# A vision tower's last feed-forward layer: one hand-written round an image, with its matrix products sorted by form

## The chip, the cores and the metric

The program runs on one core of one Trainium2 chip. The time is that of the whole program on the device, in microseconds (us), from start to end of one execution. Three executions of the kernel before took 1974.23, 1974.34 and 1977.2 us; their median is 1974.34. A further execution was taken with the hardware profiler: 1978.17 us, of which the span from the first to the last instruction is 1976.5.

The engines have short names here. PE is TensorE, which multiplies matrices; PEld is its loading of the stationary operand; DVE is VectorE, ACT is ScalarE, POOL is GpSimd; SP issues DMAs. Each engine works through its own list of instructions in order and waits at semaphores for the others. PE writes its results to PSUM, which has 8 banks of 128 x 512 numbers of 32 bits; ACT and DVE read them from there.

## What is computed

The program cuts 32 images of 3 x 256 x 256 into 256 tokens of 256 numbers each and sends them through two layers of attention and feed-forward. All numbers are float32. The change concerns the last part alone, the feed-forward of layer 1, which is itself a small attention with four heads (`NH`) and four experts (`NE`) a head:

```python
def _L1_ffn_ref(x, ...):                      # x: normalised tokens of all images
    sx = einsum('bsh,ndh->bnsd', x, hl_w) + hl_b          # 4 heads of 64
    q = einsum('bnsd,neod->bneso', sx, wq)                # one query per expert
    k = einsum('bnsd,nod->bnso', sx, wk)
    v = einsum('bnsd,nod->bnso', sx, wv)
    scores = einsum('bnesd,bntd->bnest', q, k) * d ** 0.5 + causal
    att = softmax(scores, axis=-1)
    qkv = einsum('bnest,bntd->bnesd', att, v)
    out = transpose(qkv, (0, 1, 3, 2, 4)).reshape(b, nh, s, ne * d)
    gs = softmax(einsum('bnsf,nef->bnse', out, gate_w) + gate_b, axis=-1)
    mixed = einsum('bnsed,bnse->bnsd', out.reshape(b, nh, s, ne, d), gs)
    resid = sx[arange(nh), arange(nh)]
    fx = layernorm(mixed + resid) ...                     # per head of 64
    hx = relu(fx @ fc1_w.T + fc1_b) @ fc2_w.T + fc2_b
    fout = layernorm(hx + fx, fnorm_g, fnorm_b)
    fg = softmax(fout @ fgate_w.T, axis=-1)
    return fout * fg                                      # added to the stream
```

## The kernel before

The kernel keeps all 32 images' tokens on the chip (`H`, one tile an image) and does the stages one after the other. The last stage, the feed-forward, begins at about 1275 us and ends the program. It takes one image after the other, cut into small pieces, and the pieces of several images are interleaved, so that every engine has something to do while an image's own chain waits.

What happens to an image, in order:

- `prep` -1 normalises the tokens (DVE, tile `ex`), `prep` 0 turns them feature-major (four transposes on PE, a copy to `exT` on ACT), `prep` 2 makes the heads `sx` (PE products with `w_hl`, two copies on ACT) and sends a copy with the two halves of partitions exchanged, `sw`, by two DMAs of SP. For the first four images it also makes `res`, the residual of the reference.
- `experts` multiplies the heads with `A` (query and key weights in one) and `experts_out` copies the result to `g` on ACT; `head_values` and `head_values_out` make the values `ev`; `prep` 7 also counts zeros.
- `scores` makes the scores in six steps k of two banks each; `weights` takes the exponentials of those banks on ACT (tiles `et`) and clears later keys by `affine_select` on POOL.
- `values` multiplies exponentials and values, 192 passes on PE an image in three groups, and copies eight results to `eo` on ACT.
- `post` 0 to 3: the gate's softmax, its mix of the experts (two multiplications of 128 x 1024 numbers on POOL, for the last two images on DVE), the sum and the residual `er`. `post` 15, 4, 5: a square on ACT, its sum on DVE, the power -1/2 on POOL (`head_rstd`, tile `hv`), the product on DVE. `post` 6 transposes it on PE, `post` 7 is the product with `fc1`, followed by four DMAs to the tile `both`, `post` 8 the product with `W2`. `post` 9, 10, 11, 12, 13 and 14 normalise, gate, transpose back, add and store. `post` 16 counts zeros, `post` 17 checks ranges for the last image.

All PE instructions have one helper, `mm` (L115), so the profile tells them apart by tiles. They come in three forms. *Full* products use all 128 rows and columns of PE's array: heads, `fc1`, all transposes. *Column halves* have 128 rows and 64 result columns; two such products run side by side in the two halves: `values` and `W2`. *Row halves* have 64 rows (one head of 64 is summed over) and 128 columns, also two side by side: `experts`, `head_values`, `scores`. A float32 product is two passes in the trace, a transpose one.

The order is written out by hand, for all engines. A step t does, for every image with a piece due, first the scores and experts of that step, then the early pieces, the exponentials, the other pieces by the tables `EARLY` and `PIECES`, and then the values; an image begins every six steps, so six steps are a round. `END` lists the pieces left after the last image. A bank is taken by `bank()`, in turn from a pool of eight, so the taker waits for the release of the bank taken eight times earlier.

Of the kernel before, what the change touches and what calls it, by code (L numbers as in the profile page):

```python
# [40 lines left out]
P = 128  # L41
# [38 lines left out]
def vit_tower(tc, a, out):  # L80
# [931 lines left out]
    with (  # L1012
# [4 lines left out]
        class Image:  # L1017


            def __init__(self):  # L1020
                self.p, self.t = {}, {}
# [4 lines left out]
        def prep(b, im, i):  # L1026
            if i == -1:
                im.x = normed_e(p1, b)
            if i == 0:
                im.xT = features(p1, im.x)  # L1030
            if i == 2:
                im.sx = p2.tile([P, 2, N], F32, name="sx")
                p = bank()
                for hp in range(2):
                    for k in range(2):
                        mm(p[:, hp * N : (hp + 1) * N], hl[:, k, hp * P : (hp + 1) * P], im.xT[:, k, :], k == 0, k == 1)
                for hp in range(2):
                    nc.scalar.activation(
                        im.sx[:, hp, :], p[:, hp * N : (hp + 1) * N], AF.Identity, bias=col("hl_b", hp)
                    )  # L1040

                im.sw = p2.tile([P, 2, N], F32, name="sw")
                for h in range(2):
                    nc.sync.dma_start(im.sw[halves[1 - h], :, :], im.sx[halves[h], :, :])
                im.g = p2.tile([P, NH, 2, N], F32, name="g")
                if b < NH:
                    p = bank()
                    for c in range(NC):
                        for k in range(2):
                            mm(  # L1050
                                p[:, c * HD : (c + 1) * HD], im.xT[:, k, c * P : (c + 1) * P],
                                hl[:, k, b * HD : (b + 1) * HD], k == 0, k == 1,
                            )
                    nc.vector.tensor_tensor(
                        res[:, :, b, :], p[:, 0 : NC * HD].rearrange("p (c d) -> p c d", c=NC),
                        over(row_e("hl_b")[:, b * HD : (b + 1) * HD], [P, NC, HD], 1), ALU.add,
                    )
                if b == NH - 1:
                    centred(res8, res8, NC * NH)
            if i == 7:  # L1060
                head_values_out(im)
                count_zeros(im.sx, b)
# [7 lines left out]
        def experts(im, hp):  # L1070


            ps = [bank(), bank()]
            for j in range(2):
                for s, p in zip(halves, ps):
                    mm(p[:, j * N : (j + 1) * N], A[s, hp, j * P : (j + 1) * P], im.sx[s, hp, :])
            im.pg = hp, ps

        def experts_out(im):
            hp, ps = im.pg  # L1080
            for h, p in enumerate(ps):
                nc.scalar.copy(im.g[:, 2 * hp + h, :, :].rearrange("p j n -> p (j n)"), p)  # L1082

        def head_values(im):
            im.v = p2.tile([P, NC, NH, VC], F32, name="ev")
            im.pv = [bank(), bank()]
            for c in range(NC):
                for hp in range(2):
                    o = (2 * c + hp) * VC
                    for s, p in zip(halves, im.pv):  # L1090
                        mm(p[:, o : o + VC], im.sx[s, hp, c * P : (c + 1) * P], WV[s, hp, :])

        def head_values_out(im):
# [7 lines left out]
        def scores(im, k):  # L1101


            if k == 4:
                im.o = p2.tile([P, NC * NH, 360], F32, name="eo")
# [10 lines left out]
        def weights(im, k):  # L1116

            hp, part = k // 3, k % 3
            for i, p in enumerate(im.p[k]):
# [4 lines left out]
                own = t[:, :, 0:P]  # L1124
# [4 lines left out]
                for h in range(2) if part == 2 else (part,):  # L1129
                    for j in range(2):  # L1130
                        im.t[2 * hp + h, 2 * j + i, part == 2] = t[:, 2 * (part // 2) * h + j, :]

        def values(im, j):
            for n, c in (((0, 0), (1, 0), (0, 1)), ((1, 1), (2, 0), (3, 0)), ((2, 1), (3, 1)))[j]:
                p, o = bank(), 0
                for e in range(NE):
                    x, w = TAKE[e]
                    for m in range(c + 1):
                        t = im.t[n, e, True] if m else im.t[n, e, False][:, c * P : (c + 1) * P]
                        for q in (slice(0, HD), slice(HD, P)):  # L1140
                            mm(p[q, o : o + w], t[:, q], im.v[:, m, n, x : x + w], m == 0, m == c)
                    o += w
                nc.scalar.copy(im.o[:, c * NH + n, 0:OC], p[:, 0:OC])  # L1143
# [38 lines left out]
        def post(b, im, i):  # L1182
# [37 lines left out]
            if i == (17 if b == B - 1 else 10) and b % 8 == 7:  # L1220
                check_ranges(b)
            if i == 5:
                nc.vector.tensor_tensor(im.r, im.r, over(im.rs, G8, 2), ALU.mult)
            if i == 6:
                p = feature_major(im.r.rearrange("p (c n) d -> p c (n d)", c=NC))
                im.fT = p1.tile([P, 2, N], F32, name="fxT")
                nc.scalar.activation(
                    im.fT.rearrange("p k n -> p (k n)"), p, AF.Identity, bias=col("e_b"), scale=col("e_g")
# [3 lines left out]
            if i == 7:  # L1232
                p = bank()
                mm(p, fc1, im.fT.rearrange("p k n -> p (k n)"))
                im.hx = p1.tile([P, 2, N], F32, name="hx")
                nc.scalar.activation(im.hx.rearrange("p k n -> p (k n)"), p, AF.Relu, bias=col("fc1_b"))
# [6 lines left out]
            if i == 8:  # L1243
                im.y = p2.tile([P, NC * NH, YC], F32, name="ey")
                for c in range(NC):
                    p = bank()
                    for n in range(NH):
                        for q in halves:
                            x = im.both[:, n % 2, n // 2, c * P + q.start : c * P + q.stop]
                            mm(p[q, n * YC : (n + 1) * YC], x, W2[:, n, :])  # L1250
                    nc.vector.tensor_tensor(
# [16 lines left out]
            if i == 12:  # L1268
                p = feature_major(im.r.rearrange("p (c n) d -> p c (n d)", c=NC))
                im.fT = p1.tile([P, 2, N], F32, name="foT")  # L1270
                nc.scalar.activation(
                    im.fT.rearrange("p k n -> p (k n)"), p, AF.Identity, bias=col("fn_b"), scale=col("fn_g")
# [24 lines left out]


        images = [Image() for _ in range(B)]
        SCORES, VALUES, LAST = 6, 11, 12  # L1300
        EARLY = ((32, post, 9), (22, post, 15))
        PIECES = (
            (24, post, 5), (0, prep, 0), (36, post, 12), (30, post, 16), (18, post, 1),
            (25, post, 6), (7, prep, 7), (31, post, 8), (19, post, 2),
            (38, post, 13), (2, prep, 2), (26, post, 7),
            (39, post, 14), (33, post, 10), (21, post, 3),
            (34, post, 11),
            (23, post, 4), (17, post, 0), (-1, prep, -1),
        )


        END = (
            (1, 1), (4, 12), (4, 13), (1, 2), (3, 16), (0, 0), (2, 5), (2, 6), (1, 3),
            (1, 15), (0, 1), (3, 8), (2, 7), (1, 4), (3, 9), (0, 2), (1, 5), (3, 10),
            (2, 16), (1, 6), (0, 3), (0, 15), (2, 8), (1, 7), (0, 4), (3, 11), (3, 12),
            (0, 5), (2, 9), (4, 14), (2, 10), (1, 16), (0, 6), (1, 8), (1, 9), (0, 7),
            (2, 11), (1, 10), (3, 13), (3, 14), (0, 16), (0, 8), (0, 9), (0, 10), (2, 12),
            (1, 11), (2, 13), (1, 12), (0, 11), (0, 17), (2, 14), (1, 13), (0, 12), (1, 14),
            (0, 13), (0, 14),
        )  # L1320

        def pieces(t, table):
            for step, do, i in table:
                b, r = divmod(t - step, 6)
                if r == 0 and 0 <= b < B:
                    do(b, images[b], i)

        order = tc.manual_schedule(engines={ENG.PE, ENG.DVE, ENG.Activation, ENG.Pool, ENG.SP})
        with order:
            for t in range(-1, 6 * (B - 1) + LAST):  # L1330
                active = [(images[b], t - 6 * b) for b in range(B)]
                if t % 2 == 0:
                    step = [(im, i - SCORES) for im, i in active if SCORES <= i < SCORES + 6]
                    made = [(im, i // 2 - 2) for im, i in active if i in (4, 6)]
                    for im, k in step:
                        scores(im, k)
                        scores(im, k + 1)
                    for im, hp in made:
                        experts(im, hp)
                    for im, i in active:  # L1340
                        if i == 6:
                            head_values(im)
                    pieces(t, EARLY)
                    for im, k in step:
                        weights(im, k)
                        weights(im, k + 1)
                    for im, hp in made:
                        experts_out(im)
# [401 lines left out]
```

## Time and profile before

| | us |
|---|---|
| median of three runs | 1974.34 |
| the profiled execution | 1978.17 |
| its span | 1976.5 |
| PE busy | 1933.4 (98%) |
| DVE busy | 1217.1 (62%) |
| POOL busy | 932.5 (47%) |
| ACT busy | 828.0 (42%) |
| start of the heads' products of image 5 | 1359.8 |
| of image 31 | 1888.8 |
| last score product | 1913.36 |

From image 5 to image 31 a round takes (1888.8 - 1359.8) / 26 = 20.35 us.

How it is read: busy time is the union of an engine's instructions. For PE the end of an instruction is modelled, and instructions overlap in the pipeline, so a share of 98% doesn't say that its array is well used; the distance from one start to the next is what counts. PE runs at full clock in the stage and at a lower mean (0.64) after the last score product, where it often waits.

### The profile page before, as it was taken

How to read it: one execution, taken by the hardware profiler on the slowest of the kernel's cores; microseconds unless marked ns; L12 is line 12 of the kernel's file. 1: busy time of each engine (PE TensorE's matmuls, PEld its weight loads, DVE VectorE, ACT ScalarE, POOL GpSimd, SP SyncE). 2: the span in 40 equal slices, each digit the busy share in tenths (PEclk: the TensorE clock that was granted, in tenths of full speed). 3: DMA queues.
4: the chain of work that ended last, by engine and by line, in shares of the span. 5: the costliest groups of instructions: out<-in, count | busy, mean ns of one | idle time of the engine just before them, and what ended most of it. 6: DMA issues, size and time to landing. Idle time of an engine off the chain costs nothing.

```text
span 1976.5 us, 37770 instructions
## 1 busy us (share of the span) xinstructions
PE 1933.4 (98%) x15108; PEld 1374.1 (70%) x15108; DVE 1217.1 (62%) x3225; ACT 828.0 (42%) x1549; POOL 932.5 (47%) x1072
## 2 busy tenths in 40 slices
PE   9999999999999999999999999999999999999984
PEld 7887676767666767666555555577787777778773
DVE  2335556566676655334565564536788878878886
ACT  0001312222222121222434444367777777777762
POOL 1223224343433343244334334247878787777862
PEclk9999999999999999999999999999999999999995
DMA  8550001000000142121000000001212122121212
GB/s 293 153 159 1 0 17 33 16 22 11 22 14 19 43 136 79 54 70 43 15 8 0 1 1 0 6 18 34 66 45 66 45 54 57 45 66 45 66 39 60
DMA packets 69668, 95.02 MB, mean 48 GB/s; under 512 B 8560, under 2 KB 51056, under 8 KB 69104
## 3 DMA queue, kind: packets, MB, share of 16 engines
q1 hardware_dynamic: 62768, 74.98, 13.4%
q0 software_dynamic: 6144, 16.79, 2.7%
q8 instruction: 121, 1.98, 0.4%
q10 hardware_dynamic: 576, 0.79, 0.1%
q14 instruction: 59, 0.48, 0.1%
HBM read 46.38 MB, written 20.97 MB: 34 GB/s over the span
## 4 chain that ended last, share of the span: by engine, by line
PE 94%; DVE 3%; POOL 1%; DMA 1%; ACT 1%; issue 0%; SPq 0%; ACTq 0%; DVEq 0%
PE bank L115 88%; PE bank L750 2%; PE bank L188 1%; PE bank L1279 1%; POOL eo L1205 0%; POOL hv L1157 0%; DMA patch<-in_patches_dram 0%; PE bank L229 0%; PE bank L482 0%; POOL et L1125 0%; DVE eo L1205 0%; DMA out_dram<-ex 0%; DVE six L123 0%; DVE h L827 0%; DMA sw<-sx 0%
## 5 line engine op out<-in xcount | busy, mean ns | idle before, releaser
L1125 POOL TENSOR_SCALAR_AFFINE_SELECT et<-et 128x256 f32<-128x256 f32 (+1 forms) x384 | 238.0, 651 | 34.2 <-ACT et L1122 32.4
L115 PEld LDWEIGHTS bank<-ev,et 128*64 128x64 f32 x6144 | 197.5, 136 | 33.2 <-issue 22.9
L115 PE MATMUL bank<-ev,et 128*64 128x74 f32 (+1 forms) x6144 | 210.2, 226 | 0.0
L1122 ACT ACTIVATE et<-bank 128x512 f32<-128x512 f32 x384 | 198.2, 604 | 21.4 <-PE bank L115 17.7
L115 PE MATMUL bank<-g,sx 64*128 64x512 f32 (+1 forms) x512 | 191.0, 502 | 1.4 <-ACT g L1082 1.4
L115 PE MATMUL bank<-g,sw 64*128 64x512 f32 (+1 forms) x512 | 190.0, 502 | 0.2 <-DMA sw<-sx 0.2
L115 PE MATMUL bank<-tokW,patch 128*128 128x256 f32 x768 | 168.9, 383 | 2.3 <-DMA patch<-in_patches_dram 2.3
L115 PEld LDWEIGHTS bank<-tokW,patch 128*128 128x128 f32 x768 | 147.6, 193 | 24.0 <-issue 3.2
L1205 POOL TENSOR_TENSOR eo<-eo,gate 128x1024 f32<-128x1024 f32 x60 | 114.3, 1927 | 102.3 <-DVE sm_m L1168 94.4
L115 PE MATMUL bank<-bxT,w_wuv 128*128 128x512 f32 x300 | 131.4, 592 | 0.0
L1143 ACT COPY eo<-bank 128x286 f32<-128x286 f32 x256 | 95.4, 404 | 68.0 <-PE bank L115 62.0
L148 POOL TENSOR_SCALAR rs_c<-st_c 128x4 f32<-128x4 f32 x16 | 3.1, 192 | 252.7 <-DVE st_c L124 252.7
L1157 POOL TENSOR_TENSOR hv<-hv,minus_half 128x8 f32<-128x8 f32 x64 | 119.2, 1862 | 5.3
L115 PE MATMUL bank<-wvo,dm 128*128 128x512 f32 x256 | 114.3, 599 | 0.0
L115 PE MATMUL bank<-w_wo,gT 128*128 128x256 f32 x512 | 113.1, 379 | 0.0
L115 PE MATMUL bank<-attn,bv 128*128 128x256 f32 x512 | 113.1, 379 | 0.0
L115 PE MATMUL bank<-w_w,hT 128*128 128x256 f32 x512 | 113.1, 379 | 0.0
L115 PE MATMUL bank<-xsel,w_w 128*128 128x512 f32 x256 | 111.4, 592 | 0.0
L115 PEld LDWEIGHTS bank<-attn,bv 128*128 128x128 f32 x512 | 97.2, 190 | 19.6 <-issue 6.7
L123 DVE BATCH_NORM_STATS2 six<-h 128x6 f32<-128x256 f32 x256 | 105.6, 413 | 4.4
L115 PEld LDWEIGHTS bank<-w_w,hT 128*128 128x128 f32 x512 | 96.6, 190 | 15.3 <-issue 2.9
L115 PEld LDWEIGHTS bank<-w_wo,gT 128*128 128x128 f32 x512 | 97.2, 190 | 13.2
(268 smaller groups left out, 3832.0 us busy)
## 6 DMA issues: line engine op xcount, KB each, us to landing
patch<-in_patches_dram SPq DMA_DIRECT2D x31, 768.0 KB, 4.5
sw<-sx SPq DMA_DIRECT2D x64, 128.0 KB, 2.4
both<-fxT SPq DMA_DIRECT2D x64, 128.0 KB, 2.2
both<-hx SPq DMA_DIRECT2D x64, 128.0 KB, 2.4
out_dram<-fout SPq DMA_DIRECT2D x29, 256.0 KB, 2.5
cs<-ranked SPq DMA_DIRECT2D x32, 128.0 KB, 2.0
results<-cy SPq DMA_DIRECT2D x32, 128.0 KB, 1.7
w_w<-in_w_dram SPq DMA_DIRECT2D x2, 1024.0 KB
```

The costliest lines, as they stand in the source:

```text
L115: nc.tensor.matmul(o, lhsT, rhs, start=first, stop=last)
L123: nc.vector.bn_stats(six, x)
L148: nc.gpsimd.tensor_scalar(o, var, 1.0, 1e-5, ALU.mult, ALU.add)
L188: nc.tensor.transpose(p[:, o : o + P], x[:, c, k * P : (k + 1) * P], ident)
L750: nc.tensor.transpose(p[:, o : o + P], x[:, c, k * P : (k + 1) * P], ident)
L1122: nc.scalar.activation(t, p, AF.Exp)
L1125: nc.gpsimd.affine_select(out=own, in_=own, pattern=[[0, n_e], [1, P]], compare_op=ALU.is_ge, fill=0.0, base=0, channel_multiplier=-1,)
L1143: nc.scalar.copy(im.o[:, c * NH + n, 0:OC], p[:, 0:OC])
L1157: nc.gpsimd.tensor_tensor(v, v, minus_half, ALU.pow)
L1205: (nc.vector if b > B - 3 else nc.gpsimd).tensor_tensor(im.mix[k], im.mix[k], over(im.gate[:, :, 2 * k : 2 * k + 2], [P, NC * NH, 2, HD], ...
L1279: nc.tensor.transpose(im.po[:, o : o + P], im.fT[:, k, c * P : (c + 1) * P], ident)
```

## The change

The pieces are cut finer, so that a product and the copy of its result are separate pieces, and their order is one table for a round of one image. The 59 pieces are numbered in the order in which an image needs them. `ROUND` names pairs (how many images back, piece); a round r does piece k for image r - back. PE's part of the table has all full products first (`post` 7 and 12, `post` 6 and 13, heads, the turn), then all on column halves (outputs 0 to 3, `post` 8, outputs 4 to 7), then all on row halves (experts 0, head values, experts 1, scores 2 to 5, and scores 0 and 1 of the next image). An image passes through nine rounds, from its tokens three rounds ahead to `post` 13 and 14 five rounds behind.

`weights` is split into `exponentials` (ACT) and `later_keys` (POOL), `values` into eight `outputs`, and `post` 6, 7, 8 and 12 into the PE part and a part 60, 70, 80 and 120 on ACT or DVE that reads the bank. The range check of the last image stands behind the hand-written order. What is computed, the number of instructions of each kind and the tiles' pools are the same.

```diff
-        def prep(b, im, i):
...
+        def turn(b, im):
+            im.pt = feature_major(im.x)
+
+        def turned(b, im):
+            im.xT = p1.tile([P, 2, N], F32, name="exT")
+            nc.scalar.copy(im.xT.rearrange("p k n -> p (k n)"), im.pt)
+
+        def heads(b, im):
+            p = im.ph = bank()
...
+        def heads_out(b, im):
+            im.sx = p2.tile([P, 2, N], F32, name="sx")
...
-        def weights(im, k):
-
+        def exponentials(b, im, k):
             hp, part = k // 3, k % 3
+            im.own[k] = []
             for i, p in enumerate(im.p[k]):
                 n_e = 4 if part == 2 else 2
                 t = pt.tile([P, 512], F32, name="et")
                 nc.scalar.activation(t, p, AF.Exp)
                 t = t.rearrange("p (e n) -> p e n", e=n_e)
-                own = t[:, :, 0:P]
+                im.own[k].append((t[:, :, 0:P], n_e))
...
+        def later_keys(b, im, k):
+
+            for own, n_e in im.own[k]:
                 nc.gpsimd.affine_select(
...
-        def values(im, j):
-            for n, c in (((0, 0), (1, 0), (0, 1)), ((1, 1), (2, 0), (3, 0)), ((2, 1), (3, 1)))[j]:
...
+        def outputs(b, im, j):
+            if j == 0:
+                im.o = p2.tile([P, NC * NH, 360], F32, name="eo")
+            n, c = ((0, 0), (1, 0), (0, 1), (1, 1), (2, 0), (3, 0), (2, 1), (3, 1))[j]
...
             if i == 6:
-                p = feature_major(im.r.rearrange("p (c n) d -> p c (n d)", c=NC))
+                im.pt = feature_major(im.r.rearrange("p (c n) d -> p c (n d)", c=NC))
+            if i == 60:
                 im.fT = p1.tile([P, 2, N], F32, name="fxT")
...
         PIECES = (
...
+            (tokens,), (turn,), (turned,), (heads,), (heads_out,), (experts, 0), (head_values,), (experts_out, 0),
+            (experts, 1), (experts_out, 1), (head_values_out,), (scores, 0), (scores, 1), (exponentials, 0),
+            (exponentials, 1), (heads_zero,), (later_keys, 0), (scores, 2), (scores, 3), (scores, 4), (scores, 5),
+            (exponentials, 2), (exponentials, 3), (exponentials, 4), (later_keys, 1), (exponentials, 5),
+            (later_keys, 2), (later_keys, 3), (outputs, 0), (outputs, 1), (outputs, 2), (outputs, 3),
+            (later_keys, 4), (outputs, 4), (outputs, 5), (later_keys, 5), (outputs, 6), (outputs, 7), (post, 0),
+            (post, 1), (post, 2), (post, 3), (post, 15), (post, 4), (post, 5), (post, 6), (post, 60), (post, 16),
+            (post, 7), (post, 70), (post, 8), (post, 80), (post, 9), (post, 10), (post, 11), (post, 12), (post, 120),
+            (post, 13), (post, 14),
         )
-
-
+        ROUND = (
+            (1, 39), (0, 24), (0, 25), (-3, 0), (-1, 13), (4, 54), (3, 48), (4, 55), (0, 26), (0, 27), (3, 49),
+            (-1, 14), (2, 44), (2, 45), (5, 57), (1, 40), (5, 58), (-2, 3), (2, 46), (-1, 15), (-3, 1), (4, 56),
+            (-2, 4), (0, 28), (0, 29), (-3, 2), (0, 30), (0, 31), (3, 50), (3, 51), (1, 41), (0, 32), (0, 33),
+            (0, 34), (0, 35), (3, 52), (0, 36), (3, 53), (0, 37), (-2, 5), (-2, 6), (-1, 16), (-2, 7), (0, 38),
+            (-2, 8), (-2, 9), (-1, 17), (-1, 18), (-2, 10), (1, 42), (-1, 19), (-1, 20), (2, 47), (-1, 21), (1, 43),
+            (-1, 22), (-1, 23), (-2, 11), (-2, 12),
+        )
...
+        LAST = PIECES.index((scores, 5))
+
+        def order_e():
+            for r in range(min(r for r, _ in ROUND), B + max(r for r, _ in ROUND)):
+                for back, k in ROUND:
+                    b = r - back
+                    if 0 <= b < B:
+                        yield b, k
+                        if (b, k) == (B - 1, LAST):
+                            yield from ((B - 1 - last, k) for last, k in END)
+                            return
+
+        with tc.manual_schedule(engines={ENG.PE, ENG.DVE, ENG.Activation, ENG.Pool, ENG.SP}):
+            for b, k in order_e():
+                do, *i = PIECES[k]
+                do(b, images[b], *i)
+        check_ranges(B - 1)
```

`END` has a new list of the pieces left after the last score product of image 31: 93 pairs of images 26 to 31, in place of 56.

## The prediction

> **What bounds the kernel now.** I read the shares first (PE 98%), then busy time by stretch, then the PE timeline of one round, then the rows of single tiles. By stretch (columns: stretch, length, busy of PE, PEld, DVE, ACT, POOL with instruction counts, granted clock, DMA share, GB/s):
>
> ```profile
> 1300.00:1880.00 580.00, 579.35 (x8924) 457.94 (x8922) 449.54 (x1072) 447.80 (x965) 438.35 (x508) 1.00 0.21 51
> 1502.26:1522.61 20.35, 20.35 (x316) 16.26 (x315) 17.42 (x41) 15.63 (x35) 15.12 (x19) 1.00 0.21 54
> 1913.36:1976.50 63.14, 32.02 (x384) 23.97 (x380) 45.30 (x124) 17.48 (x37) 18.26 (x20) 0.64 0.18 49
> ```
>
> The first line is the feed-forward in its steady part: PE lacks 0.65 us of 580. The second is one image: PE is full for all of its 20.35 us, at full clock, and DVE is next at 17.42. The third starts at the last product of a score and ends the run: there the last image's own chain decides, and PE is half idle. So from about 1275 to 1913 us the time is PE's list of work and nothing else; what shortens it must be in that list. The PE timeline shows what:
>
> ```profile
> 1506.72 0.43 PE L115 MATMUL bank<-ev,et 128*64 128x74 f32 x8
> 1507.08 0.69 PE L115 MATMUL bank<-g,sw 64*128 64x512 f32 x1
> 1507.61 0.59 PE L115 MATMUL bank<-g,sw 64*128 64x512 f32 x1
> 1508.05 0.38 PE L115 MATMUL bank<-g,sw 64*128 64x256 f32 x1
> ...
> 1521.18 0.59 PE L115 MATMUL bank<-g,sw 64*128 64x512 f32 x1
> 1521.60 0.59 PE L115 MATMUL bank<-g,sx 64*128 64x512 f32 x1
> 1522.13 0.55 PE L1279 MATMUL bank<-ident,foT 128*128 128x128 f32 x3
> ```
>
> Read the starts, since the ends are modelled. A pass of 512 columns takes 0.43 us (1507.61 to 1508.05, 1521.18 to 1521.60); the first pass after products of another form takes 0.53 (1507.08 to 1507.61), and the step from a row-half pass to a full transpose also takes 0.53 instead of 0.43. Nothing is waited for there; the change of form costs.
>
> **What the change removes.** Prices by kind, from starts in this round (first start after the change, plus what the second is late, each less the same step without a change):
> - full to column halves: 522 for 430 ns, then 115 for 64: 145 ns
> - column to row halves: 158 for 57, then 533 for 429: 205 ns
> - row to column halves: 306 for 209, then 115 for 64: 148 ns
> - row halves to full: 202 for 81, then 166 for 109 (178 ns); at the other place 520 for 422, then 165 for 109 (154 ns).
>
> An image has 2, 3, 1 and 2 of them: 290 + 615 + 148 + 332 = 1.385 us, so 18.96 of the 20.35 us are products. After the change it has one full to column (145), one column to row (205) and one row to full. That last one is followed by fc1's 512 columns; three rows early in the stage, where a wide full product follows a row half, show 519 for 422 and 320 for 216, so 200 ns. Sum 0.55. **A round without waits is 19.51 us, 0.84 less.** For the total I count changes of form in the order of PE's instructions, from the stage's first transpose to the last score product: 253 before (62 full-column, 93 column-row, 31 row-column, 64 row-full, 3 full-row), 96 after (31, 31, 0, 32, 2). That is 9.0 + 19.1 + 4.6 + 10.6 + 0.6 = 43.9 us against 4.5 + 6.4 + 6.4 + 0.4 = 17.7: **26.2 us saved.** The products themselves are the same, 5,297 in both.
>
> **What it moves.** Behind the last score product now lie one fc1 (2 x 0.43) and one set of foT transposes (4 x 0.11) more: 1.3 us leave the full part and go where PE is busy 32 of 63 us, at no cost. The last image's chain (exponentials, selects, eight outputs, post 0 to 14, the DMAs of `both`, out) has the same links; I keep its 63.1 us, with 4 to either side for the new order of the other images' pieces. The range check of the last image, now written after the hand order, was built in among DVE's waits before the last two stores: nothing, or its two operations of 0.64 us.
>
> Banks: the round takes 34 of them through 8 in turn. The densest part is the row halves, 18 banks in 0.86 + 0.90 + 0.86 + 6 x 0.86 = 7.8 us. At one place a rule speaks against this: the Trainium skill, "TensorEngine Tiling (Array Packing)", PSUM Bottleneck, warns that tiling speeds the products and not the emptying of PSUM. By the rule ACT would set the row part. By rows: after the second expert product ACT has two copies of `g` (0.47 apart), one square (0.47 more) and then exponentials 0.48 apart (four in 2.04 at 604 each, with one 0.2 us gate). Its eighth ends 6 us after that product; the transposes of post 6, which take that bank up again, come 6.66 us after it. Slack 0.6 us or more; I go by the rows: 0.
>
> SP's queue keeps seven issues an image: `sw` is sent by the heads' copies and read by scores 0 at the end of the same round's row part, some 12 us later (it landed in 2.4); `both` has the transposes of that round and the first outputs of the next, about 5 us against 2.4. POOL: selects 4 and 5 stand behind post 2's two mixes (3.8 us), so they end some 6 us after the heads' first product; outputs 6, their last reader, start at about 8 (heads 1.73, turn 0.44, four outputs and post 8). Nothing for either.
>
> **The wait that it adds** is DVE's. In the new order post 15 (the square) stands on ACT after the second experts' copies, and DVE then has post 4, post 1, the next normalisation, post 11 and only then post 5, which PE's post 6 needs. Count from the end of the second expert product. ACT: 0.2 latency + 0.47 + 0.47 + 0.63 = 1.77. DVE: reduce 0.67, add, max, subtract 0.56, two `ex` 0.82, `enorm` 0.69, `lg` 0.18 to 0.39, four small ones 0.71 to 1.01, `er` 0.69 to 1.1: from 4.3 to 5.3, with the medians of the rows 5.0. Ready at 6.1 to 7.0, likely 6.8. PE gets there after six score pairs (5.16), a change (0.20), fc1 (0.86) and post 12 (0.44): 6.66. The wait is 0 to 0.4 us a round. Its size hangs on DVE's rows beside POOL:
>
> ```profile
> L1223 DVE TENSOR_TENSOR er<-er,hv x32: 680/876/884, 1333.9 to 1942.3; 128x512 f32<-128x512 f32 x32
> L1170 DVE TENSOR_TENSOR fgate<-fgate,sm_m x32: 160/1735/1740, 1377.5 to 1967.0; 128x8 f32<-128x8 f32 x32
> L1289 DVE TENSOR_TENSOR fout<-fout,h x29: 691/1037/1131, 1381.2 to 1966.0; 128x512 f32<-128x512 f32 x29
> ```
>
> (minimum/median/maximum ns). An eight-column multiply takes 1735 ns because it stands beside POOL's mix of 1927. The Trainium skill, "SBUF — State Buffer", SBUF: two separate sides, says that a DVE operation with two SBUF inputs and a GpSimd one exclude each other for the whole instruction. By the rule `er`, which in the new order meets the 512-column selects of `later_keys`(2), loses a whole one of them (0.64): 1.33 us, a wait of 0.6, some 16 us in all. The row says 876 for 693 alone, 0.18 lost beside a 256-column select (404 alone), since part of it is over when `er` comes. I scale the row to the longer select, 0.2 to 0.4 lost, and take **0.2 us of wait in 27 rounds (31 less the first four, which have no such piece), 5.4 us**; ends 0 and 16. The mix itself costs nothing: `fgate` stood behind it before, and `fout`, which now comes while the second mix runs (1.1 us more), is followed by the wait of post 80 for its products, where DVE has 1 us left. Without that cover it would be late for `two`, and er again.
>
> Ramp and other waits: 2 us, for four rounds with other neighbours.
>
> **Sum**, against the profiled execution of 1978.2 us (span 1976.5): -26.2 - 1.3 + 5.4 + 2 = -20.1, so 1958.1. That execution stood 3.8 over the median of the three shown (1974.34), hence **1954 us**.
>
> **Rivals.**
> - No wait at all: POOL's selects keep out of `er`'s way. -27.5: 1947. For it: `er` has 0.5 us in hand where its neighbours are alone; against: DVE's idle time falls from 2.9 to 2.1 us a round.
> - DVE and POOL set the round. If lost locks add up to 0.7 us (the rule's case, and one more small operation behind a select), 27 x 0.7 = 19 us are given back: 1966. For it: 17.4 of 19.5 us busy; against: the locks that one part loses are partly idle time elsewhere.
> - Slower: `er` or its predecessors fall behind a mix. The place is post 2's mix, 1.93 us long twice, now issued right after post 5; a small DVE operation that meets it takes 1735 for 167, so 1.57 us. In every round that is 27 x 1.57 = 42 us, against 27.5: 1989. It decides from 1.0 us a round. Against it: post 2 stands behind `er` on DVE itself, so a mix must be a round late.
> - The change doesn't do what it says: a bank or a tile ties the order so that PE stops at each part's first product. Speaks against: the slack of 0.6 us or more above. 1974.
>
> **Chances.** Forecast 0.60 (own range 1948 to 1962), no wait 0.12, DVE and POOL 0.18, slower 0.07, nothing 0.03. The range from 1944 to 1968 leaves out the slower case, nothing, and the edges. A measurement of this kernel tells 0.2%, 4 us, from no change: faster takes the first three less a little of the third, 0.88; same 0.05; slower 0.07.
>
> **What would show it.** Right: three changes of form a round, each at 0.15 to 0.2 us; starts of the heads' products 19.6 to 19.9 us apart; PE's only regular wait before the transposes of `er`, put down to DVE; the last score product near 1893 us and 63 us behind it. Wrong: a wait of PE on ACT's exponentials or on `later_keys`; a round over 20.2; a tail of 70 us.

## The result and the profile after

| | before | after |
|---|---|---|
| median of four runs each, same chip | 1975.77 us (1974.23 to 1978.75) | 1951.15 us (1948.89 to 1953.11) |
| ratio of the times | | 0.9873, 95% interval 0.9854 to 0.9892 |
| the profiled execution, its span | 1978.17, 1976.5 | 1953.11, 1951.4 |
| start of the first heads' product of the stage | 1274.8 | 1275.3 |
| one round, median | 20.34 | 19.57 |
| last score product | 1913.4 | 1889.4 |
| from there to the end | 63.1 | 62.0 |

The changed kernel is 1.3% faster. Of the 25.1 us between the two spans, 24.4 lie between the first heads' product and the last score product (638.5 against 614.1), 1.1 behind it, and 0.5 were lost before the stage, where nothing was changed.

Busy time by stretch, after (stretch, length, busy of PE, PEld, DVE, ACT, POOL with counts, granted clock, DMA share, GB/s): the steady part, one round, and the end from the last score product on.

```profile
1300.00:1860.00 560.00, 557.82 (x8906) 455.37 (x8901) 455.42 (x1081) 442.50 (x968) 386.21 (x505) 1.00 0.21 52
1486.60:1506.18 19.58, 19.58 (x317) 16.02 (x316) 17.71 (x42) 15.59 (x35) 14.31 (x19) 1.00 0.22 57
1889.43:1951.40 61.97, 32.77 (x390) 24.45 (x386) 44.74 (x117) 18.27 (x38) 20.81 (x25) 0.70 0.23 61
```

PE is as full as before, in a round that is 0.77 us shorter. DVE has 17.71 us of work in 19.58, so its idle time fell from 2.9 to 1.9 us. Next is the timeline of one change of form, rows to full, with PE, the weight loads (PEld) and DVE's `er` (columns: start, length, engine, line, operation, tiles; in brackets the idle time before it):

```profile
1503.36 0.59 PE L115 MATMUL bank<-g,sw 64*128 64x512 f32 x1
1503.37 0.59 PE L115 MATMUL bank<-g,sx 64*128 64x512 f32 x1
...
1503.89 0.30 PEld L115 LDWEIGHTS bank<-fxT,w_fc 128*128 128x128 f32 x2 [0.76 <-ACT gate L1174]
1503.89 1.16 DVE L1233 TENSOR_TENSOR er<-er,hv 128x512 f32<-128x512 f32 x1
1503.89 1.13 PE L115 MATMUL bank<-fxT,w_fc 128*128 128x512 f32 x2
1504.42 0.14 PEld L750 LDWEIGHTS bank<-ident,enorm 128*128 128x128 f32 x1 [0.24 <-issue]
1504.85 0.60 PE L750 MATMUL bank<-ident,enorm 128*128 128x128 f32 x4
...
1505.18 0.36 PEld L750 LDWEIGHTS bank<-ident,er 128*128 128x128 f32 x3
...
1505.29 0.38 PE L750 MATMUL bank<-ident,er 128*128 128x128 f32 x2
```

Two things are to be seen. Within one form a weight load starts one product ahead: that of `enorm` at 1504.42 for a product at 1504.85. At the change the load of `w_fc` starts with its own product, at 1503.89; that product comes 0.52 us after the last row pair (1503.37), where a pass of 512 columns takes 0.43, and its two passes take 0.96 us to the next start (1504.85), where two take 0.86. Together that is the 0.2 us of this change of form, and the change removes five like it from a round. And `er` ends at 1503.89 + 1.16 = 1505.05, just ahead of the load that needs it (1505.18).

### The profile page after: what moved, and what is told of

Read it like the earlier page. It is cut to its first block, busy times and chain, and to the rows that moved or that the text cites. A ratio compares the mean times of both kernels' runs of the same rounds, so it can differ in the third digit from the quotient of the medians.

```text
span 1951.4 us, 37903 instructions
## 1 busy us (share of the span) xinstructions
PE 1908.1 (98%) x15108; PEld 1370.5 (70%) x15108; DVE 1209.3 (62%) x3225; ACT 821.0 (42%) x1549; POOL 877.5 (45%) x1072
## 4 chain that ended last, share of the span: by engine, by line
PE 95%; DVE 2%; POOL 1%; DMA 1%; ACT 0%; issue 0%; SPq 0%; ACTq 0%; DVEq 0%
PE bank L115 90%; PE bank L750 2%; PE bank L188 1%; PE bank L1294 1%; DMA patch<-in_patches_dram 0%; POOL hv L1167 0%; PE bank L229 0%; PE bank L482 0%; POOL et L1136 0%; DVE six L123 0%; DMA both<-hx 0%; POOL eo L1215 0%; DVE enorm L1273 0%; DVE ranges L1228 0%; DVE h L827 0%
## 5 line engine op out<-in xcount | busy, mean ns | idle before, releaser
L1136 POOL TENSOR_SCALAR_AFFINE_SELECT et<-et 128x256 f32<-128x256 f32 (+1 forms) x384 | 200.2, 553 | 19.4 <-ACT et L1126 18.8
L115 PE MATMUL bank<-ev,et 128*64 128x74 f32 (+1 forms) x6144 | 205.7, 227 | 1.9 <-POOL et L1136 1.9
L115 PE MATMUL bank<-g,sx 64*128 64x512 f32 (+1 forms) x512 | 170.7, 483 | 0.0
L115 PE MATMUL bank<-g,sw 64*128 64x512 f32 (+1 forms) x512 | 170.3, 483 | 0.0
L115 PEld LDWEIGHTS bank<-tokW,patch 128*128 128x128 f32 x768 | 147.7, 193 | 24.4 <-issue 3.5
L1153 ACT COPY eo<-bank 128x286 f32<-128x286 f32 x256 | 101.9, 402 | 91.1 <-PE bank L115 78.7
L115 PEld LDWEIGHTS bank<-g,sw 64*128 64x128 f32 x512 | 95.7, 187 | 33.0 <-issue 21.9
L1167 POOL TENSOR_TENSOR hv<-hv,minus_half 128x8 f32<-128x8 f32 x64 | 108.8, 1699 | 5.3
L115 PEld LDWEIGHTS bank<-attn,bv 128*128 128x128 f32 x512 | 97.2, 190 | 19.6 <-issue 6.9
L115 PEld LDWEIGHTS bank<-g,sx 64*128 64x128 f32 x512 | 95.7, 187 | 19.4 <-issue 14.8
```

Source lines behind the costliest of these rows:

```text
L115: nc.tensor.matmul(o, lhsT, rhs, start=first, stop=last)
L1136: nc.gpsimd.affine_select(out=own, in_=own, pattern=[[0, n_e], [1, P]], compare_op=ALU.is_ge, fill=0.0, base=0, channel_multiplier=-1,)
L1167: nc.gpsimd.tensor_tensor(v, v, minus_half, ALU.pow)
```

## The experiments

The times are medians of 4 to 12 runs. A round is read as the distance between the first heads' products of two images, where the median over the steady rounds repeats to 0.01 us. The stage, from the first heads' product to the last score product, is given too. `ROUND` is the table of the changed kernel; a pair is (images back, piece).

The ratio of each run is to runs of the kernel before on the same chip.

| run | changes of form a round | round, us | stage, us | time, us | ratio to before, 95% |
|---|---|---|---|---|---|
| before | 8 | 20.34 | 638.5 | 1975.8 | |
| changed kernel | 3 | 19.57 | 614.1 | 1951.2 | 0.9854 to 0.9892 |
| turn among the outputs | 5 | 19.87 | 622.6 | 1960.7 | 0.9912 to 0.9948 |
| and post 13 | 7 | 20.17 | 632.1 | 1966.5 | 0.9943 to 0.9972 |
| and outputs split | 9 | 20.52 | 638.9 | 1977.1 | 0.9997 to 1.0015 |
| seven banks | 3 | 19.66 | 616.7 | 1959.6 | 0.9904 to 0.9937 |
| one addition before `er` | 3 | 20.54 | 639.8 | 1980.6 | 1.0012 to 1.0031 |
| two additions before `er` | 3 | 21.36 | 661.9 | 2002.3 | 1.0115 to 1.0149 |
| cheaper changes | 3 | 19.61 | 618.4 | 1954.2 | 0.9868 to 0.9901 |
| mix ahead of selects | 3 | 20.50 | 645.4 | 1981.1 | 1.0008 to 1.0031 |
| changed kernel, again | 3 | 19.57 | 614.6 | 1950.7 | 0.9851 to 0.9885 |
| `er` out of line | 3 | 19.52 | 612.7 | 1950.3 | 0.9856 to 0.9889 |

### Is it the form? The changes put back by twos

The products, the copies and the fine pieces stay; only places in `ROUND` move. First the turn, (-3, 1), goes between two outputs:

```diff
-            ... (-1, 15), (-3, 1), (4, 56), (-2, 4), (0, 28), (0, 29), (-3, 2), (0, 30), ...
+            ... (-1, 15), (4, 56), (-2, 4), (0, 28), (0, 29), (-3, 1), (-3, 2), (0, 30), ...
```

> The changed kernel with one piece moved: the turn (four transposes, a full product) stands between outputs 2 and 3 instead of behind the heads, so PE has two changes of form more a round (full to column halves and column halves to full); the same products, the same copies. Theory (the time is PE's list, and a change of form costs 0.145 to 0.2 us): 0.29 to 0.35 us a round, rounds of 19.86 to 19.92 instead of 19.57, some 31 times: 1951 + 9 to 11 = 1960 to 1962 us. Rival (the gain came from finer pieces, other neighbours and fewer waits, not from the forms): rounds of 19.57 and 1951.

Then post 13 and its reader, (5, 57) and (5, 58), go between (0, 28) and (0, 29):

> As the one before, and post 13 with its reader moved to between outputs 0 and 1: four changes of form more a round than the changed kernel. Theory: twice the dose, 0.58 to 0.7 us a round, rounds of 20.15 to 20.27, 1951 + 18 to 22 = 1969 to 1973 us. Rival: rounds of 19.57 and 1951; if only one of the two moves costs time, it is a wait at that place and not the change of form.

Then outputs 6 and 7, (0, 36) and (0, 37), go behind the first experts' product, (-2, 5):

> As the one before, and outputs 6 and 7 moved behind the first experts' product: a row part before and after them, two changes more (row to column 0.148, column to row 0.205), six more in all, nine a round where the kernel before had eight. Theory: 0.35 us a round on top, rounds of 20.5 to 20.62, 1951 + 29 to 33 = 1980 to 1984 us, above the kernel before, with all of the finer pieces and the new order of the other engines still in place. Rival: 1951 to 1955.

The rounds were 19.87, 20.17 and 20.52 us: steps of 0.302, 0.300 and 0.351. The two kinds that were known from before sum to 0.353 for the last step, and a column-to-full change, which no earlier row showed, costs 0.302 - 0.145 = 0.157. PE's timeline of the third run shows two groups of full products among the outputs, with four changes of form:

```profile
1512.31 0.72 PE L115 MATMUL bank<-ev,et 128*64 128x74 f32 x16
1512.96 0.66 PE L1294 MATMUL bank<-ident,foT 128*128 128x128 f32 x4
1513.55 0.72 PE L115 MATMUL bank<-ev,et 128*64 128x74 f32 x16
1514.20 0.66 PE L750 MATMUL bank<-ident,ex 128*128 128x128 f32 x4
1514.78 2.21 PE L115 MATMUL bank<-ev,et 128*64 128x74 f32 x64
```

Four transposes take 0.59 us here from their start to the next group's (1512.96 to 1513.55), and 0.44 in a run of full products. In their steady part no wait was recorded on PE in any of the three runs. That alone says little, since the run with the mix ahead of the selects, further down, loses 0.93 us a round and has no recorded wait either. But counted from the start of one group of products to the start of the next, only what stands beside a new change became longer. In the first run the heads take 1.82 us for 1.73, the transposes of the turn 0.585 for 0.530, and the outputs ahead of `W2` 3.18 for 3.03: the 0.30 of the round. In the third run the experts and head values grow from 2.72 to 2.92 and the last four outputs from 3.08 to 3.23. `W2`, the scores, `fc1` and the transposes of `enorm` and `er`, beside which nothing was moved, take 8.04 us together in all four kernels. With nine changes a round the kernel is back at the time of before (1977.1 and 1976.4 us on the same chip), with all of the finer pieces and the new order of the other engines in place. So the gain is the changes of form, and the rival falls. The second and the third whole time came out below what was expected: I counted 31 rounds, and only some 27 have all of the moved pieces; 27 x 0.60 and 27 x 0.95 on 1951.2 give 1967.4 and 1976.9. The stages of the profiled executions are 8.5, 18.0 and 24.8 us longer than the changed kernel's; the 18.0 are more than 27 x 0.60 since one early round of that run took 21.90 us, where the changed kernel's took 20.30.

### Are the banks near their limit?

```diff
-    ppool = top.enter_context(tc.tile_pool(name="ppool", bufs=8, space=PSUM))
+    ppool = top.enter_context(tc.tile_pool(name="ppool", bufs=7, space=PSUM))
```

> The changed kernel with seven PSUM banks in the pool instead of eight, in the whole program, so only the stage's rounds and its length are compared (start of the heads of image 7 to 31). Every bank has to be free one take (some 0.43 us in the row part) earlier. Theory of the prediction (0.6 us or more of slack between ACT's copies and the next taker): 0.2 us of wait a round at most, rounds of 19.57 to 19.8. Rival (ACT's emptying of the banks sets the row part, eight banks are just enough): 0.43 us at several takes of the part, rounds of 20.5 or more.

Rounds of 19.66: a bank less costs 0.09 us, all of it in the scores (5.35 us for 5.26). The transposes of `post` 6, ahead of which the prediction read 0.6 us of slack from ACT's rows, come no later. The rest of the loss in that run's time lies in earlier stages: its first heads' product starts at 1280.4.

### What is next in line? More work before `er`

```diff
             if i == 5:
+                for _ in range(1):
+                    extra = p1.tile([P, 2 * N], F32, name="junk")
+                    nc.vector.tensor_tensor(extra.rearrange("p (g d) -> p g d", d=HD), im.r, res8, ALU.add)
                 nc.vector.tensor_tensor(im.r, im.r, over(im.rs, G8, 2), ALU.mult)
```

> The changed kernel with one more DVE addition of 128x512 (from the tile er and res, into a scratch tile; 0.69 us alone) ahead of the product er of post 5. In the trace of the changed kernel er ends 0.2 us before its transposes start, so theory (er is the next thing in line behind PE, with 0.2 us in hand): the added operation takes er's place beside POOL's select (1.15 us), er then runs in 0.69, and PE waits 0.69 - 0.2 = 0.5 us a round, rounds of 20.05 and some 15 us more, 1966. Rival (DVE is off PE's path altogether, with 2 us idle in a round): rounds of 19.57 and 1951.

The second run has `range(2)`:

> As the one before, with two such additions. Theory: 2 x 0.69 - 0.2 = 1.2 us of wait a round, rounds of 20.75, some 36 us more, 1987, slower than the kernel before although it has three changes of form a round. Rival: 1951 to 1955; if one addition costs nothing and two do, the time in hand was sized too small.

Both cost more than I had expected: 0.97 and 1.79 us a round. From the run with one addition, what PE waited for, and the rows of the two operations (minimum/median/maximum in ns):

```profile
PE bank L750 <- DVE sm_m L1178: 17.1, 22, 0.8
```

```profile
L1235 DVE TENSOR_TENSOR junk<-er,res x23: 1153/1156/1159, 1407.8 to 1859.7; 128x512 f32<-128x512 f32 x23
L1236 DVE TENSOR_TENSOR er<-er,hv x22: 931/932/934, 1409.1 to 1840.4; 128x512 f32<-128x512 f32 x22
```

PE waits before the transposes of `er` in every round (`sm_m` L1178 is only DVE's next operation; the row of the wait names the one that came last). Two errors of the expectation show. `er` did not fall back to 0.69 us: with the addition in its old place it met the next select and took 0.93. And the time in hand is not 0.2 us. Where PE waits, its first transpose starts 0.147 us after the recorded end of `er`. In the changed kernel it starts 0.239 after it. The difference, **0.09 us a round**, is all that `er` has in hand. With it the sum comes out: 0.93 and a gap of 0.1 ahead of it, less 0.09, is 0.94; the step from the first transpose to the second, 0.136 for 0.109, adds 0.03, and 0.97 was measured.

### The slower rival: the mix ahead of the selects

```diff
-            ... (4, 55), (0, 26), (0, 27), (3, 49), (-1, 14), (2, 44), (2, 45), (5, 57), (1, 40), (5, 58), ...
+            ... (4, 55), (1, 40), (0, 26), (0, 27), (3, 49), (-1, 14), (2, 44), (2, 45), (5, 57), (5, 58), ...
```

> The slower rival of the prediction, put in on purpose: post 2 (the rest of the gate's softmax and POOL's two mixes, 3.8 us) stands ahead of the selects of later keys 2 and of er, so that er meets a mix and not a select, and the selects come 3.8 us later. Rival's price: er 1.57 us late, less 0.2 in hand, 1.4 us a round from er alone, rounds of 20.9 to 21 and 1990, above the kernel before. Other outcome, if er starts ahead of the mix and keeps POOL waiting: no wait for er beyond 0.7 us; then the selects' delay is the larger part, as a wait of outputs for POOL.

Rounds of 20.50, 0.93 more than the changed kernel. DVE's and POOL's timelines of one round:

```profile
1575.99 0.19 DVE L1212 TENSOR_TENSOR gate<-gate,ranges 128x32 f32<-128x32 f32 x1
1576.10 0.68 DVE L1233 TENSOR_TENSOR er<-er,hv 128x512 f32<-128x512 f32 x1
```

```profile
1576.33 4.12 POOL L1215 TENSOR_TENSOR eo<-eo,gate 128x1024 f32<-128x1024 f32 x2 [0.99 <-DVE gate L1212]
```

And the two mixes of a round of the changed kernel:

```profile
1486.66 3.81 POOL L1215 TENSOR_TENSOR eo<-eo,gate 128x1024 f32<-128x1024 f32 x2
```

The last small operation of the gate releases the mix, but `er` follows it on DVE at once, starts 0.23 us ahead of the mix and takes 0.68; now it is the mix that is held up (two take 4.12 us, where they took 3.81 in the changed kernel). Of the 0.93 us, 0.25 are lost before the transposes of `er` (four operations of the gate's softmax now stand ahead of it), and 0.68 in the outputs, whose first group takes 3.71 us for 3.03: their selects start at 1580.41, behind the mixes. So the other outcome came: a 1.93 us mix does not delay `er` in this order either, and the loss comes from the selects behind it. By its whole time the kernel is slower than the one before, by 0.2%, and by another way than the rival named.

### What remains to be had

> The changed kernel with its three changes of form at cheaper places: post 12 (transposes) ahead of post 7, since row halves to a wide full product cost 0.201 and to transposes 0.154 to 0.178, and the head values ahead of the first experts (column to row 0.158 + 0.177 for 0.057 + 0.112, so 0.166, for 0.204). Theory: 0.06 to 0.08 us a round less, rounds of 19.49 to 19.51, 2 us less, 1949. Rival (the head values' banks, which DVE empties late, come to be wanted two takes earlier): a wait of 0.04 to 0.4 us a round, 19.55 to 19.9.

Here (4, 55) stands ahead of (3, 48), and (-2, 6) ahead of (-2, 5). Rounds of 19.61, and 19.85 in each round with a range check. The head values ahead of the experts bring nothing: the three groups together take 2.724 us in both orders, for what the entry saves is lost at the step between head values and experts. The transposes come in cheaper, but PE now waits for `er`, 0.147 us after its end again, and the two operations of the range check show too. The 19.49 to 19.51 of the theory did not come, and the rival's number came for another reason than its own: the head values' products, with the price of the change (0.854 + 0.104), take 0.958 us and wait for no bank. So I took `er` out of the line:

```diff
-            ... (4, 54), (3, 48), (4, 55), (0, 26), (0, 27), (3, 49), (-1, 14), (2, 44), (2, 45), (5, 57), ...
+            ... (4, 54), (4, 55), (3, 48), (0, 26), (0, 27), (3, 49), (-1, 14), (2, 44), (5, 57), (2, 45), ...
```

> The changed kernel itself, to stand beside the next one on the same chip: 1951 us, rounds of 19.57.

> The changed kernel with post 12 ahead of post 7 (row halves to transposes instead of to a wide product) and post 6, the reader of er, behind post 13, so that er has 0.44 us more. In the run with the cheaper changes the transposes came first and PE then waited for er. Theory (of what is left only er was in the way): the step into the full products costs 0.046 us less (0.492 + 0.861 for 0.963 + 0.436) and nothing is waited for, rounds of 19.52, 1.4 us less than the changed kernel over the stage. Rival (another wait, on a bank or on fxT, stands just behind er): rounds of 19.57 to 19.7.

PE's timeline of a change of form in this kernel:

```profile
1498.97 0.59 PE L115 MATMUL bank<-g,sx 64*128 64x512 f32 x1
1499.49 0.66 PE L750 MATMUL bank<-ident,enorm 128*128 128x128 f32 x4
1499.98 1.02 PE L115 MATMUL bank<-fxT,w_fc 128*128 128x512 f32 x2
1500.84 0.60 PE L1294 MATMUL bank<-ident,foT 128*128 128x128 f32 x4
1501.28 0.60 PE L750 MATMUL bank<-ident,er 128*128 128x128 f32 x4
```

`enorm` and `w_fc` take 0.49 and 0.86 us, as expected, and nothing is waited for: rounds of 19.525, which is 0.045 less. Over the stage that is 1.4 to 1.9 us (612.7 for 614.1 and 614.6). The medians, 1950.3 and 1950.7, can't tell it from the changed kernel, so I don't call it faster as a whole. It shows that nothing else of the old order stands within these 0.045 us behind `er`.

## Why the prediction was right, step by step

The forecast of 1954 us is 2.9 above the measured median; its own range of 1948 to 1962 held it. Against the profiled execution the sum said 1958.1, and 1953.1 was measured: 20.1 us were forecast to go and 25.1 went. That the median looks nearer is in part luck, since the kernel before had a median of 1974.34 in the three executions shown and of 1975.77 in four. By the profiled executions the rival without a wait (27.5 us less, 1950.7) was nearer than the forecast.

- **PE's list bounds the stage, and changes of form are what the change takes out of it.** Right, by the dose of two, four and six. The three kinds that remain measured as priced: 0.145, 0.204 and 0.201, together 0.55. The Trainium skill, "TensorEngine Tiling (Array Packing)", says under Key Properties that a change of tiling mode drains the engine, without a price; here it is 0.145 to 0.205 us.
- **26.2 us saved and 1.3 moved behind the last score product.** 27.5 in all; the stage fell by 24.4. The 3.1 between them stand against 7.4 of waits in the sum.
- **The wait for `er`, 0.2 us in 27 rounds.** This term was mis-sized: no such wait came, and it makes up the forecast's excess of 5.0 us; the other terms were off by 1.1, 0.5 and -1.1. The PE side was exact: 6.66 us from the end of the second expert product to the transposes were predicted, and 1498.63 to 1505.29 were measured. DVE was early: ready after 6.42 where I took 6.8. The twelve DVE operations ahead of `er` took 3.43 us from start to start (1500.46 to 1503.89) instead of 4.1 (5.0 less the 0.88 of `er`). Some 0.4 of that are shorter operations than in the rows of before (their durations there sum to 3.71); the other 0.3 are the sum of durations itself, since DVE starts an operation that does not read the result of the one ahead some 0.08 us before the recorded end of that one. `er` itself was longer than I took it, 1.16 for 0.88. And the count left out the 0.147 us that pass between the end of `er` and its transposes: 6.66 less 6.42 less 0.15 are the 0.09 in hand. The rival without a wait had the right outcome here for a wrong reason: the selects do not keep out of `er`'s way.
- **What `er` loses beside the long select.** Between row and rule. Three DVE rows of the changed kernel, against 1735, 876 and 1037 before:

```profile
L1180 DVE TENSOR_TENSOR fgate<-fgate,sm_m x32: 164/1937/1942, 1388.8 to 1942.1; 128x8 f32<-128x8 f32 x32
```

```profile
L1233 DVE TENSOR_TENSOR er<-er,hv x32: 679/1154/1158, 1328.2 to 1921.0; 128x512 f32<-128x512 f32 x32
```

```profile
L1304 DVE TENSOR_TENSOR fout<-fout,h x29: 692/1585/1621, 1391.6 to 1939.2; 128x512 f32<-128x512 f32 x29
```

  `er` takes 1154 for 693 alone: 0.46 lost, where I had scaled the old row to 0.2 to 0.4 and the rule of the Trainium skill, "SBUF — State Buffer", SBUF: two separate sides, by which `er` waits for the whole select, gave 0.64. Both rows fit one sum that the scaling missed: when `er` started, 0.33 us of the select were left before the change and 0.61 after it, and it lost 0.15 less than that both times. `fgate` and `fout` lose more than before as well; as the prediction had it, that fell into DVE's idle time before post 80 and cost nothing.
- **The rule on PSUM evacuation costs nothing here.** Right: even with a bank less the transposes that the prediction had looked at came no later, and the scores lost 0.09 us.
- **Ramp and other waits, 2 us.** This term was too small: 3.1 us were measured, the only loss there is. In 26 steady rounds 0.06 each (19.57 for 18.96 + 0.55 = 19.51), 1.6 us, lie at the steps between experts and head values, which now stand between two experts' products: their three groups take 0.968 + 0.854 + 0.902 less 0.104 of the change of form, 2.62 us, for 0.960 + 0.863 + 0.952 less 0.218, 2.56, before. That leaves some 1.5 us for the first and last rounds. PE's recorded waits in the stage are about that much longer: 4.1 us, none of them in the steady rounds, against 2.3 in the kernel before. These four:

```profile
PE bank L115 <- POOL et L1136: 1.9, 3, 1.0
PE bank L115 <- DMA both<-hx: 1.2, 1, 1.2
PE bank L115 <- ACT exT L1034: 0.7, 1, 0.7
PE bank L750 <- DVE sm_m L1178: 0.3, 1, 0.3
```

  The first is for POOL's selects in the first rounds, the second for the DMA of `both` in the last one, at 1882 us. For both places the prediction had nothing, from their times in a steady round, and in the steady rounds it was right.
- **A tail of 63.1 us, kept.** 62.0, and 60.9 to 61.4 in five other runs of its `END`, those with the forms put back, with seven banks, and the repeat. Right within its bounds.
- **The signs named.** Three changes a round: seen. Rounds of 19.6 to 19.9: 19.57. A regular wait for `er`: not there. Last score product near 1893: 1889.4.

What was left open: a change of form is paid when the weight load is no longer a product ahead, as the timeline shows, but whether it is the load, or the emptying of the array, that costs the time was not tried.

## What to carry to other kernels

Where one engine is full and waits for nothing, count what stands between its instructions: here 8 changes of operand form a round, at 0.15 to 0.2 us each, were 7% of the time, and a new order removed five of them. The saving is exact only while the next engine keeps up: measure how much it has in hand against a run in which the reader does wait, and count by starts and not by summed durations. Here 0.24 us lay between the end of `er` and its reader; 0.15 of them pass even when the reader waits, so 0.09 us in hand looked like 0.2. A kernel that has just become tighter has a new place that decides; one added operation of 0.7 us on DVE, which has idle time in every round, took the whole gain back.

## What the runs showed of the hardware

- Between DVE and POOL the one that starts first holds up the other, in both directions: `er` beside a select takes 1.154 us for 0.69, and started 0.23 us ahead of a mix it takes 0.68, and the mix then 2.25 for 1.93. What the later one loses is what was left of the holder by its record when it started, less 0.14 to 0.15 us (medians of steady rounds; lost is measured against 0.692 us alone for `er` and `fout` and 0.165 for `fgate`):

| kernel | DVE operation | behind | left of it, us | lost, us |
|---|---|---|---|---|
| two additions before `er` | `er` | select | 0.163 | 0.012 |
| before | `er` | select | 0.334 | 0.184 |
| one addition before `er` | `er` | select | 0.389 | 0.241 |
| changed kernel | `er` | select | 0.613 | 0.464 |
| changed kernel | `fout` | mix | 1.037 | 0.893 |
| changed kernel | `fgate` | mix | 1.915 | 1.774 |

  The power on POOL (`hv`, 1.67 us) does not hold DVE up: in the changed kernel `enorm` starts with 0.93 us of it left and takes 0.683 us.
- From the recorded end of a DVE result to the start of the PE product that waits for it were 0.147 us, in four kernels; its weight load starts 0.117 us after that end.
- The part of the program before the stage, with the same instructions, took 1271.1 to 1276.0 us in the profiled runs with eight banks, while a round repeated to 0.01 us. A change of a few us in one stage is read from that stage, not from whole times.
